# A shorter quotient for the FFN weight, value products behind the scores of a later item, projections and joint norms two slots later

## The chip, the cores and the metric

The kernel runs on one core of one Trainium2 chip, in one launch. The metric is the device time of one execution in microseconds (us); lower is better. PE is the matrix engine, DVE the vector engine, ACT the scalar engine, POOL the GpSimd engine; SP is the engine that issues nearly all DMAs here.

## What is computed

x has shape (4, 4096, 512) in float32. Three residual steps follow one another:

```python
x = x + 0.5 * ffn(layernorm(x))
x = x + attention(layernorm(x))
x = x + 0.5 * ffn(layernorm(x))
```

`ffn` quantises its input and its 512 x 512 weight in blocks of 32 to a 6-bit grid (scale = largest absolute value / 7.5, nearest grid value, ties to the lower one), multiplies the dequantised matrices and adds a bias:

```python
scales = maximum(max(abs(blocks), -1) / 7.5, 1e-30)
q = nearest_on_grid(blocks / scales)
out = (xq * xs) @ (wq * ws).T + bias
```

`attention` has 16 heads of 32 and a window of 13 neighbours (clipped at the ends of the sequence) with a relative position bias per head; it projects to q, k and v, takes the softmax of q k + bias over the 13 neighbours, multiplies by v and projects the result with `proj_w`.

## The kernel before

The 16384 rows are cut into 128 tiles of 128 rows. Every product with a weight is done with both operands split into a high and a low float16 half; `product` (L152) issues 12 matmuls of 128 x 512 for it. The weights sit transposed in `wt`, put there in a setup that quantises the FFN weight `fw` and splits all weights.

Four tiles make a group; a group and a quarter of the heads make an item, so there are 128 items too, and a tile and an item take the same number of steps. The steps are:

- `first_half(t)`: the first FFN product (`pmf`), its addition to x on DVE (L280), the statistics of the second norm (L181), its factors on POOL, the normalised tile on ACT, its low half on DVE and a transposing DMA into `x2` (L206).
- `values(t)`: the v product (`pmv`), which goes to DRAM (L317) and comes back as stacks of overlapping windows (`load_stack`, L441).
- `project_qk(m)`: two products (`pmqk`); DVE subtracts the high halves (L391), ACT spreads q (L398).
- `softmax(m)`: 64 to 72 small matmuls for the scores (`ps`, L466), then DVE, POOL and ACT in turn; in the end the probabilities are transposed by a DMA (`pT`, L535).
- `attend(m)`: the value products (`pv`, L557), 64 to 72 small matmuls; their result goes to a ring of rows (L584 on ACT, L590 on DVE).
- `project_out(t)`: the product `pmo` from the ring, its addition to x (L603) and the statistics of the third norm.
- `quantised_norms(slot)`: the norm and quantisation ahead of an FFN product. It runs for one tile, or jointly for two, the third norm of a tile and the first norm of the tile 15 further on. Its stages, one per slot: factors (POOL, L187 to L196), normalised tile (ACT, L234), block scales (DVE, L240 to L245), scaling (POOL, L247), rounding to 8 bits (ACT, L250), scaling back (POOL, L252), high half (ACT, L201), low half (DVE, L205) with the transposing DMA to `xT` (SP, L206).
- `second_half(t)`: the second FFN product (a `pmf` again, from `xT`), its addition (L280) and the store (L609).

The order on every engine is written out by hand. Time is cut into slots; a step is entered into a slot with a rank, and goes on in a later slot with the rank that its `yield` names. Within a slot the lower rank comes first, and equal ranks in the order of entry. Each engine executes its instructions in that order; the setup alone is ordered by a planner, up to the point where the manual order begins. Tile t and item m are `STEP` = 7 slots behind their predecessors:

```python
for _, stage in sorted(slots.pop(slot, ()), key=lambda e: e[0]):
    for n, rank in stage:
        begin(slot + n, stage, rank)
        break
```

The results of products share three PSUM banks in turn (`ps_m`); scores have four banks, value products one. The last tiles have slots of their own (`out_slot`, `second_slot`), and eight second halves (`HELD`) are kept back for the end.

Of the kernel before, what the change touches and what calls it, by code (L numbers as in the profile page):

```python
# [37 lines left out]
P = 128  # L38
# [12 lines left out]
QB = 32  # L51
Q_MAX = 7.5
Q_EPS = 1e-30
LN_EPS = 1e-5

F8_SCALE = 64.0
BELOW_ONE = 1.0 - 2.0 ** -24
MASKED = -1e38
XS = 4.0
PS = 1024.0  # L60
# [4 lines left out]
def macaron_kernel(  # L65
# [25 lines left out]
    const = ctx.enter_context(tc.tile_pool(name="const", bufs=1))  # L91
# [13 lines left out]
    nudge = const.tile([P, 1], F32, name="nudge")  # L105
    nc.gpsimd.memset(nudge, -(2.0 ** -28) * (1 + 2.0 ** -10))

    least = const.tile([P, 2 * NB], F32, name="least")
    nc.vector.memset(least, F8_SCALE * XS * Q_EPS)
    p_scale = const.tile([P, MAXB], F32, name="p_scale")  # L110
# [26 lines left out]
    def tie_to_lower(t):  # L137

        nc.vector.scalar_tensor_tensor(t, t, BELOW_ONE, t, ALU.mult, ALU.min)
        ti = t.bitcast(I32)
        nc.vector.tensor_scalar(ti, ti, 1, None, ALU.bitwise_or)

    def product(pm, lhs, rhs):

        n = 0
        for a, b in ((0, 1), (1, 0), (0, 0)):  # L150
            for c in range(KC):
                nc.tensor.matmul(  # L152
                    pm, lhs(a, c), rhs(b, c), start=(n == 0), stop=(n == 3 * KC - 1)
                )
                n += 1
# [7 lines left out]
    def begin(slot, stage, rank=5):  # L163
        slots.setdefault(slot, []).append((rank, stage))
# [185 lines left out]
    def row_of(h):  # L350

        return h // 2 * 2 * QR + h % 2

    n_items = n_batch * NG * KC
# [240 lines left out]
    def project_out(t, slot):  # L595

        r = t * P % RING
        pm = ps_m.tile([P, dim], F32, tag="mm", name=f"pmo_{t}")
        product(
            pm, lambda s, c: ring[:, s, c, r : r + P], lambda s, c: wt[:, s, c, PO : PO + dim]  # L600
        )
        yield 1, 8
        nc.vector.scalar_tensor_tensor(xs[t], pm, cp, xs[t], ALU.mult, ALU.add)  # L603
        moments(slot, t, "n3")

    def second_half(t):

        yield from ffn(t, "f2")
        nc.sync.dma_start(out=of[t * P : (t + 1) * P, :], in_=xs.pop(t))  # L609


    EARLY = 3
    STEP = 7

    F1, V, QK, SC, PV, OUT, F2 = 5, 2 * STEP + 6, 5 * STEP + 3, 6 * STEP, 8 * STEP + 3, 13 * STEP + 2, 12

    def add_bias(t, b):
        nc.gpsimd.tensor_tensor(xs[t], xs[t], b, ALU.add)  # L618
# [1 line left out]
    def one(f, *args):  # L620
        f(*args)
        return
        yield
# [3 lines left out]
    HELD = range(NT - 15, NT - 7)  # L627
    LAST = NT - GROUP - 1

    def out_slot(t):  # L630


        i = t - LAST
        if i >= 0:
            return (n_items - 1) * STEP + PV + 3 + 2 * i
        if i >= 1 - GROUP:
            return LAST * STEP + PV + 21 + 4 * i
        return t * STEP + OUT

    def second_slot(t):  # L640

        i = t - LAST
        if t in HELD:
            return (n_items - 1) * STEP + PV - (16, 13, 10, 6, 5, 4, 3, 2)[t - HELD[0]]
        if i in (-2, -1):
            return out_slot(NT - 1) + 3 + i
        return out_slot(t) + F2

    for t in range(NT):
        k = t * STEP  # L650
        sooner = (0, 2, 5, STEP)[t] if t <= EARLY else 0
        begin(k - 18 - (STEP if t == EARLY else 0), one(load, t), 0)
        slot = k - 10 - (10 if t == EARLY else 0)
        enlist(slot, t, "n1")
        if not 0 < t < EARLY:
            begin(slot - 1, one(moments, slot, t, "n1"), 1)
        begin(k + F1 - sooner, first_half(t))
        begin(k + V, values(t))
        begin(k + F1 - sooner, one(add_bias, t, half_ffn_b), 8)
        at = out_slot(t)  # L660
        begin(at - 5, one(add_bias, t, after_b), 8)
        enlist(at + 2, t, "n3")
        begin(at, project_out(t, at + 2))
        begin(at + 6 if t < LAST else second_slot(t) - 2, one(add_bias, t, half_ffn_b), 8)
        begin(second_slot(t), second_half(t))
    for slot in together:
# [2 lines left out]
    for m in range(n_items):  # L669
        k = m * STEP  # L670
        begin(k + QK, project_qk(m))
        begin(k + SC, softmax(m), 6)
        begin(k + PV, attend(m), 6)
    for n in range(n_batch * NG):
        k = n * GROUP * STEP
        b, g = divmod(n, NG)
# [4 lines left out]
    with tc.tile_pool(name="setup", bufs=1) as sp, tc.tile_pool(name="scratch", bufs=2) as scr:  # L681
        ident = sp.tile([P, P], F32, name="ident")
        make_identity(nc, ident)
        fw = sp.tile([P, KC, dim], F32, name="fw")
# [20 lines left out]
        for o in chunks:  # L705
            w, i = (qkv_w, o) if o < 3 * KC else (proj_w, o - 3 * KC)
# [14 lines left out]
        up = sp.tile([P, 5], F32, name="up")  # L721
# [40 lines left out]

        def small(name):
            return sp.tile([P, KC * NB], F32, name=name)

        w_abs, w_sc, w_hi, w_lo, w_r = (
            small(s) for s in ("w_abs", "w_sc", "w_hi", "w_lo", "w_r")
        )  # L770

        def split_scale():
            nc.vector.tensor_scalar(
                w_hi.bitcast(I32), w_sc.bitcast(I32), -4096, None, ALU.bitwise_and
            )
            nc.vector.tensor_tensor(w_lo, w_sc, w_hi, ALU.subtract)
# [17 lines left out]
        def large(name, o, dt=F32):  # L794
            return scr.tile(
                [P, NB, QB], dt, tag=name, bufs=3 if name == "wu_" else KC, name=f"{name}{o}"
            )

        for o in range(KC):
            fwb = blocks(fw[:, o, :])  # L800

            def per(t):
                return bc(t[:, o * NB : (o + 1) * NB], QB)
# [12 lines left out]
            nc.scalar.activation(  # L816
                w8.rearrange("p n q -> p (n q)"), q0f, AF.Copy, scale=1.0 / F8_SCALE,
                saturate=False,
            )
# [64 lines left out]
        for turned in (0, 2):  # L884
            for h in range(4):
                at = row_of(h ^ turned)
# [41 lines left out]
        slot = first  # L928
# [49 lines left out]
```

## Time and profile before

| | us |
|---|---|
| median of 3 runs | 2313.0 |
| lowest and highest | 2311.24, 2313.52 |
| the profiled execution, its time | 2312.25 |
| its span, first to last instruction | 2310.5 |
| PE busy | 2211.1 (96%) |
| DVE busy | 2044.8 (88%) |
| POOL busy | 1988.3 (86%) |
| ACT busy | 1695.5 (73%) |

Busy times are sums over one profiled execution. Matmuls overlap, so the length shown for a row of matmuls ends a little after the next row may start; distances from start to start are the better measure. A line number is that of the kernel's source, and an arrow `<-` in brackets names what ended a wait.

### The profile page before, as it was taken

How to read it: one execution, taken by the hardware profiler on the slowest of the kernel's cores; microseconds unless marked ns; L12 is line 12 of the kernel's file. 1: busy time of each engine (PE TensorE's matmuls, PEld its weight loads, DVE VectorE, ACT ScalarE, POOL GpSimd, SP SyncE). 2: the span in 40 equal slices, each digit the busy share in tenths (PEclk: the TensorE clock that was granted, in tenths of full speed). 3: DMA queues.
4: the chain of work that ended last, by engine and by line, in shares of the span. 5: the costliest groups of instructions: out<-in, count | busy, mean ns of one | idle time of the engine just before them, and what ended most of it. 6: DMA issues, size and time to landing. Idle time of an engine off the chain costs nothing.

```text
span 2310.5 us, 65475 instructions
## 1 busy us (share of the span) xinstructions
PE 2211.1 (96%) x26771; PEld 1052.0 (46%) x26771; DVE 2044.8 (88%) x3797; ACT 1695.5 (73%) x2544; POOL 1988.3 (86%) x2017
## 2 busy tenths in 40 slices
PE   0799999999999999999999999999999999999978
PEld 0244444444444444444444444444444444444433
DVE  8799998998988989989989899899898998998775
ACT  4588777777777777777777777777777777777752
POOL 6488988888988888888888898888898889888776
PEclk9999999999999999999999999999999999999999
DMA  5788888788877888888878888888787888887764
GB/s 153 156 167 160 162 162 159 156 163 162 154 158 157 158 163 157 160 161 159 158 156 160 158 160 166 155 154 161 159 159 157 160 158 165 156 157 148 138 109 107
DMA packets 926213, 359.61 MB, mean 156 GB/s; under 512 B 719452, under 2 KB 890328, under 8 KB 925912
## 3 DMA queue, kind: packets, MB, share of 16 engines
q1 hardware_dynamic: 925568, 354.90, 79.3%
q8 instruction: 209, 3.42, 0.6%
q14 instruction: 92, 0.75, 0.1%
q10 hardware_dynamic: 344, 0.53, 0.1%
HBM read 110.26 MB, written 67.29 MB: 77 GB/s over the span
## 4 chain that ended last, share of the span: by engine, by line
PE 89%; DVE 6%; POOL 2%; ACT 1%; DMA 1%; issue 1%; SPq 0%; POOLq 0%; DVEq 0%; ACTq 0%
PE pmqk L152 28%; PE pmf L152 27%; PE pmo L152 14%; PE pmv L152 13%; PE ps L466 4%; PE pv L557 3%; DVE stn L181 1%; DVE hlq L205 0%; ACT qk L398 0%; DVE sc L240 0%; DVE x L280 0%; DVE fw L810 0%; DVE hln L205 0%; DVE whl L840 0%; DMA fw<-in_L_ffn_weight_dram 0%
## 5 line engine op out<-in xcount | busy, mean ns | idle before, releaser
L152 PE MATMUL pmf<-wt,xT 128*128 128x512 f16 x3048 | 701.3, 380 | 9.0 <-DMA xT<-hlq 7.7
L152 PE MATMUL pmqk<-x,wt 128*128 128x512 f16 x3072 | 705.8, 379 | 0.3 <-DVE after_b L876 0.3
L152 PEld LDWEIGHTS <-xT 128*128 128x128 f16 x3048 | 297.9, 98 | 372.7 <-DMA xT<-hlq 13.1
L152 PEld LDWEIGHTS <-wt 128*128 128x128 f16 x3072 | 289.7, 98 | 335.6 <-issue 0.9
L247 POOL TENSOR_TENSOR yq<-yq,r 128x1024 f32<-128x1024 f32 (+1 forms) x141 | 247.1, 1753 | 133.9 <-DVE r L245 120.4
L152 PE MATMUL pmv<-wt,x 128*128 128x512 f16 x1536 | 354.0, 380 | 6.0 <-DMA x<-hln 3.3
L152 PE MATMUL pmo<-wt,ring 128*128 128x512 f16 x1536 | 356.1, 382 | 0.0
L398 ACT ACTIVATE qk<-qf,parity 128x1024 f16<-128x1024 f16 x256 | 349.3, 1431 | 0.0
L618 POOL TENSOR_TENSOR x<-x,half_ffn_b 128x512 f32<-128x512 f32 x256 | 327.7, 1280 | 0.0
L280 DVE SCALAR_TENSOR_TENSOR x<-pmf,coef,x 128x512 f32<-128x512 f32 x256 | 179.8, 702 | 144.5 <-PE pmf L152 142.2
L584 ACT ACTIVATE ring<-pv 128x510 f16<-128x510 f32 (+7 forms) x176 | 78.7, 475 | 297.6 <-PE pv L557 229.1
L181 DVE BATCH_NORM_STATS2 stn<-x 128x6 f32<-128x512 f32 x384 | 265.2, 691 | 8.9 <-DMA x<-in_L_attn_x_dram 0.2
L252 POOL TENSOR_TENSOR yq<-q,sc 128x1024 f32<-128x1024 fp8e4 (+1 forms) x141 | 246.6, 1749 | 1.5 <-ACT q L250 1.5
L152 PEld LDWEIGHTS <-x 128*128 128x128 f16 x1536 | 150.5, 98 | 188.9 <-issue 5.0
L250 ACT ACTIVATE q<-yq,nudge 128x1024 fp8e4<-128x1024 f32 (+1 forms) x141 | 150.0, 1064 | 116.7 <-POOL yq L247 108.5
L152 PEld LDWEIGHTS <-ring 128*128 128x128 f16 x1536 | 141.0, 98 | 159.9 <-issue 3.9
L526 POOL TENSOR_TENSOR sf<-sf,total 128x714 f32<-128x714 f32 (+2 forms) x128 | 178.7, 1396 | 37.1 <-ACT yq L234 21.6
L234 ACT ACTIVATE yq<-x,nbq,rsq 128x512 f32<-128x512 f32 x254 | 193.0, 803 | 17.1 <-POOL nbq L193 14.4
L533 POOL TENSOR_TENSOR p<-sf,p 128x714 f16<-128x714 f32 (+2 forms) x128 | 192.5, 1504 | 0.0
L517 POOL TENSOR_TENSOR sf<-sf,top 128x714 f32<-128x714 f32 (+2 forms) x128 | 181.5, 1418 | 3.8 <-DVE top L515 3.6
L205 DVE TENSOR_TENSOR hlq<-yq,hlq 128x1024 f16<-128x1024 f32 (+1 forms) x141 | 170.6, 1210 | 8.1 <-ACT hlq L201 6.9
L618 POOL TENSOR_TENSOR x<-x,after_b 128x512 f32<-128x512 f32 x128 | 162.4, 1269 | 0.0
(155 smaller groups left out, 3494.4 us busy)
## 6 DMA issues: line engine op xcount, KB each, us to landing
vs<-vd SPq DMA_DIRECT2D x144, 357.0 KB
x<-in_L_attn_x_dram SPq DMA_DIRECT2D x128, 256.0 KB
vd<-vt SPq DMA_DIRECT2D x128, 256.0 KB
out_dram<-x SPq DMA_DIRECT2D x128, 256.0 KB
vs<-vd SPq DMA_DIRECT2D x24, 378.0 KB
vs<-vd SPq DMA_DIRECT2D x24, 315.0 KB
rows<-in_L_attn_qkv_w_dram SPq DMA_DIRECT2D x12, 256.0 KB
xT<-hlq SPq DMA_TRANSPOSE x141
```

The costliest lines, as they stand in the source:

```text
L152: nc.tensor.matmul(pm, lhs(a, c), rhs(b, c), start=(n == 0), stop=(n == 3 * KC - 1))
L181: nc.vector.bn_stats(st, xs[t])
L205: nc.vector.tensor_tensor(hl[:, :, 1, :], y, hl[:, :, 0, :], ALU.subtract)
L234: nc.scalar.activation(y[:, u], xs[t], AF.Identity, bias=nb[:, u : u + 1], scale=rs[:, u : u + 1])
L247: nc.gpsimd.tensor_tensor(yb, yb, bc(r, QB), ALU.mult)
L252: nc.gpsimd.tensor_tensor(yb, q8.rearrange("p u (n q) -> p (u n) q", q=QB), bc(sc, QB), ALU.mult)
L280: nc.vector.scalar_tensor_tensor(xs[t], pm, cf, xs[t], ALU.mult, ALU.add)
L398: nc.scalar.activation(to, whole[0], AF.Copy, scale=parity[:, e : e + 1])
L517: nc.gpsimd.tensor_tensor(s, s, bc(top[:, :n], KN), ALU.subtract)
L526: nc.gpsimd.tensor_tensor(s, s, bc(total[:, :n], KN), ALU.mult)
L533: nc.gpsimd.tensor_tensor(p[:, :n, KN : 2 * KN], s, ph, ALU.subtract)
L618: nc.gpsimd.tensor_tensor(xs[t], xs[t], b, ALU.add)
```

## The change

In the setup the quotient of the FFN weight is shortened. Before, it was built from a reciprocal, a float16 first guess and two corrections with split scales, and ties were moved to the lower value by integer operations. After, the weight is multiplied by the reciprocal of its scale, and a small negative bias in ACT's rounding decides the ties; the multiplication back is on DVE and no longer on POOL.

In the order, with slots counted from 7 x the number of the tile or item: the value products of an item go from slot 59 to slot 63, which is the slot of the scores of the item three ahead, with a rank behind them (the last three items stay at 59). `project_out` goes from slot 93 to 95 with rank 7 in place of 5; `second_half` stays 12 slots behind it. The joint norms go two slots later as well (the first norm of a tile from slot -10 to -8), so the two norms stay together. For the last tiles the constants are rewritten so that most of them keep their slots.

```diff
+    w_nudge = const.tile([P, 1], F32, name="w_nudge")
+    nc.gpsimd.memset(w_nudge, -(2.0 ** -27) * (1 + 2.0 ** -10))
...
-    F1, V, QK, SC, PV, OUT, F2 = 5, 2 * STEP + 6, 5 * STEP + 3, 6 * STEP, 8 * STEP + 3, 13 * STEP + 2, 12
+    F1, V, QK, SC, PV, OUT, F2 = 5, 2 * STEP + 6, 5 * STEP + 3, 6 * STEP, 9 * STEP, 13 * STEP + 4, 12
+
+    LAST_PV = (n_items - 1) * STEP + 8 * STEP + 3
...
-            return (n_items - 1) * STEP + PV + 3 + 2 * i
+            return LAST_PV + 3 + 2 * i
         if i >= 1 - GROUP:
-            return LAST * STEP + PV + 21 + 4 * i
+            return LAST * STEP + 82 + 4 * i
...
-            return (n_items - 1) * STEP + PV - (16, 13, 10, 6, 5, 4, 3, 2)[t - HELD[0]]
+            return LAST_PV - (16, 13, 10, 6, 5, 4, 3, 2)[t - HELD[0]]
...
-        slot = k - 10 - (10 if t == EARLY else 0)
+        slot = k - (8 if t > EARLY else 18 if t == EARLY else 10)
...
-        begin(at, project_out(t, at + 2))
+        begin(at, project_out(t, at + 2), 7)
...
         begin(k + SC, softmax(m), 6)
-        begin(k + PV, attend(m), 6)
+        begin(k + (PV if m < n_items - 3 else PV - 4), attend(m), 7)
...
         for o in range(KC):
             nc.vector.tensor_reduce(
-                w_abs[:, o * NB : (o + 1) * NB], blocks(fw[:, o, :]), AX.X, ALU.max,
+                w_sc[:, o * NB : (o + 1) * NB], blocks(fw[:, o, :]), AX.X, ALU.max,
                 apply_absolute_value=True,
             )
-        nc.vector.tensor_scalar(w_sc, w_abs, 1.0 / Q_MAX, None, ALU.mult)
-        split_scale()
-        nc.vector.scalar_tensor_tensor(w_abs, w_hi, -Q_MAX, w_abs, ALU.mult, ALU.add)
-        nc.vector.scalar_tensor_tensor(w_abs, w_lo, -Q_MAX, w_abs, ALU.mult, ALU.add)
-        nc.vector.scalar_tensor_tensor(w_sc, w_abs, 1.0 / Q_MAX, w_sc, ALU.mult, ALU.add)
-        nc.vector.tensor_scalar(w_sc, w_sc, Q_EPS, None, ALU.max)
+        nc.vector.tensor_scalar(
+            w_sc, w_sc, F8_SCALE / Q_MAX, F8_SCALE * Q_EPS, ALU.mult, ALU.max
+        )
         nc.vector.reciprocal(w_r, w_sc)
-        split_scale()
-        w_back = small("w_back")
-        nc.vector.tensor_scalar(w_back, w_sc, up[:, 4:5], F8_SCALE, ALU.mult, ALU.mult)
...
         for o in range(KC):
             fwb = blocks(fw[:, o, :])
-            qh, q0 = large("wqh_", o, F16), large("wq0_", o)
-            nc.vector.tensor_tensor(qh, fwb, per(w_r), ALU.mult)
-            for i, b in enumerate((w_hi, w_lo)):
-                u = large("wu_", f"{o}_{i}")
-                nc.gpsimd.tensor_tensor(u, qh, per(b), ALU.mult)
-                nc.vector.tensor_tensor(fwb, fwb, u, ALU.subtract)
-            nc.vector.tensor_tensor(q0, fwb, per(w_r), ALU.mult)
-            nc.vector.tensor_tensor(q0, q0, qh, ALU.add)
-            q0f = q0.rearrange("p n q -> p (n q)")
-            tie_to_lower(q0f)
-            w8 = large("w8_", o, F8)
-            nc.scalar.activation(
-                w8.rearrange("p n q -> p (n q)"), q0f, AF.Copy, scale=1.0 / F8_SCALE,
-                saturate=False,
-            )
-            nc.gpsimd.tensor_tensor(fwb, w8, per(w_back), ALU.mult)
+            nc.vector.tensor_tensor(fwb, fwb, per(w_r, o), ALU.mult)
+        nc.vector.tensor_scalar(w_back, w_sc, up[:, 4:5], None, ALU.mult)
+        for o in range(KC):
+            w8 = scr.tile([P, dim], F8, tag="w8_", bufs=KC, name=f"w8_{o}")
+            nc.scalar.activation(w8, fw[:, o, :], AF.Identity, bias=w_nudge, saturate=False)
+            nc.vector.tensor_tensor(blocks(fw[:, o, :]), blocks(w8), per(w_back, o), ALU.mult)
             hl = scr.tile([P, 2, dim], F16, tag="whl", bufs=4, name=f"whlf{o}")
             nc.scalar.copy(hl[:, 0, :], fw[:, o, :])
             nc.vector.tensor_tensor(hl[:, 1, :], fw[:, o, :], hl[:, 0, :], ALU.subtract)
```

`tie_to_lower` was one DVE operation that multiplied by a number just below one and took the minimum (L143) and one that set the lowest bit (L145).

More of the change, by code (lines that the diff above doesn't have):

```diff
@@ L56 @@
 F8_SCALE = 64.0
-BELOW_ONE = 1.0 - 2.0 ** -24
 MASKED = -1e38
@@ L135, in blocks @@
         return t.rearrange("p (n q) -> p n q", q=QB)
[L137 to L145, printed above, removed]
     def product(pm, lhs, rhs):
@@ L761, in put_weights @@
             )
[L765 to L769, printed above, removed]
-        )
-        def split_scale():
-            nc.vector.tensor_scalar(
-                w_hi.bitcast(I32), w_sc.bitcast(I32), -4096, None, ALU.bitwise_and
-            )
-            nc.vector.tensor_tensor(w_lo, w_sc, w_hi, ALU.subtract)
+        w_sc, w_r, w_back = (
+            sp.tile([P, KC * NB], F32, name=name) for name in ("w_sc", "w_r", "w_back")
+        )
@@ L787, in macaron_kernel @@
-        nc.vector.scalar_tensor_tensor(w_sc, w_abs, 1.0 / Q_MAX, w_sc, ALU.mult, ALU.add)
-        nc.vector.tensor_scalar(w_sc, w_sc, Q_EPS, None, ALU.max)
-        nc.vector.reciprocal(w_r, w_sc)
-        split_scale()
-        w_back = small("w_back")
-        nc.vector.tensor_scalar(w_back, w_sc, up[:, 4:5], F8_SCALE, ALU.mult, ALU.mult)
[L794 to L797, printed above, removed]
+        nc.vector.tensor_scalar(
+            w_sc, w_sc, F8_SCALE / Q_MAX, F8_SCALE * Q_EPS, ALU.mult, ALU.max
+        )
@@ L799, in macaron_kernel, with per @@
+        nc.vector.reciprocal(w_r, w_sc)
+        def per(t, o):
+            return bc(t[:, o * NB : (o + 1) * NB], QB)
         for o in range(KC):
             fwb = blocks(fw[:, o, :])
-            def per(t):
-                return bc(t[:, o * NB : (o + 1) * NB], QB)
-            qh, q0 = large("wqh_", o, F16), large("wq0_", o)
-            nc.vector.tensor_tensor(qh, fwb, per(w_r), ALU.mult)
-            for i, b in enumerate((w_hi, w_lo)):
-                u = large("wu_", f"{o}_{i}")
-                nc.gpsimd.tensor_tensor(u, qh, per(b), ALU.mult)
-                nc.vector.tensor_tensor(fwb, fwb, u, ALU.subtract)
@@ L811, in macaron_kernel @@
-            nc.vector.tensor_tensor(q0, fwb, per(w_r), ALU.mult)
-            nc.vector.tensor_tensor(q0, q0, qh, ALU.add)
-            q0f = q0.rearrange("p n q -> p (n q)")
-            tie_to_lower(q0f)
-            w8 = large("w8_", o, F8)
-            nc.scalar.activation(
-                w8.rearrange("p n q -> p (n q)"), q0f, AF.Copy, scale=1.0 / F8_SCALE,
-                saturate=False,
-            )
-            nc.gpsimd.tensor_tensor(fwb, w8, per(w_back), ALU.mult)
+            nc.vector.tensor_tensor(fwb, fwb, per(w_r, o), ALU.mult)
```

## The prediction

> **What bounds the kernel now.** I read the page's busy shares first, then the engines' busy time by stretch, then PE's timeline over one item, then DVE's and SP's for the same item, and last the chain at both ends of the span.
>
> ```profile
> PE 2211.1 (96%) x26771; PEld 1052.0 (46%) x26771; DVE 2044.8 (88%) x3797; ACT 1695.5 (73%) x2544; POOL 1988.3 (86%) x2017
> ```
> ```profile
> 0.00:40.00 40.00, 1.55 (x5) 0.84 (x5) 32.53 (x70) 18.34 (x48) 27.46 (x49) 1.00 0.54 181
> ...
> 1000.00:1400.00 400.00, 400.00 (x4907) 191.18 (x4906) 359.35 (x662) 303.17 (x444) 356.94 (x352) 1.00 0.82 159
> ```
>
> From 260 to 2160 us PE is busy in every microsecond and its waits in that window are none. DVE has 90% there, POOL 89%, the DMA engines 82%. So the middle is PE's, with little to spare elsewhere; only the first 60 us (PE works for 3 of them) and the last 150 us wait for others. One item on PE (columns: start, length, engine, line, operation, out<-in):
>
> ```profile
> 1002.02 0.81 PE L466 MATMUL ps<-qk 64*64 64x84 f16 x68
> 1002.76 2.76 PE L152 MATMUL pmo<-wt,ring 128*128 128x512 f16 x12
> 1005.36 2.75 PE L152 MATMUL pmqk<-x,wt 128*128 128x512 f16 x12
> 1008.05 0.69 PE L557 MATMUL pv<-pT,vs 126*32 126x30 f16 x68
> 1008.67 2.76 PE L152 MATMUL pmqk<-x,wt 128*128 128x512 f16 x12
> 1011.27 2.75 PE L152 MATMUL pmf<-wt,xT 128*128 128x512 f16 x12
> 1013.86 2.75 PE L152 MATMUL pmv<-wt,x 128*128 128x512 f16 x12
> 1016.45 2.75 PE L152 MATMUL pmf<-wt,xT 128*128 128x512 f16 x12
> 1019.14 0.80 PE L466 MATMUL ps<-qk 64*64 64x84 f16 x68
> ```
>
> Start to start, a product of 12 matmuls takes 2.59 to 2.60; in front of scores (ps) or value products (pv) it takes 2.69, so entering the small tiles costs 0.09. Scores take 0.74, value products 0.62. An item is 1019.14 - 1002.02 = 17.12, or 17.11 by the mean of its neighbours. The first pmf is first_half, the second is second_half, 15 tiles behind.
>
> DVE in the same item, and the landing of a joint norm's transpose (SP's issue, and the product that waited for it in the ramp):
>
> ```profile
> 1002.13 0.75 DVE L280 SCALAR_TENSOR_TENSOR x<-pmf,coef,x 128x512 f32<-128x512 f32 x1 [1.19 <-PE pmf L152]
> ...
> 1006.50 0.72 DVE L603 SCALAR_TENSOR_TENSOR x<-pmo,coef,x 128x512 f32<-128x512 f32 x1
> 1007.25 0.69 DVE L181 BATCH_NORM_STATS2 stn<-x 128x6 f32<-128x512 f32 x1
> 1007.98 0.18 DVE L182 BATCH_NORM_AGGREGATE mv<-stn 128x2 f32<-128x6 f32 x1
> 1008.08 1.21 DVE L205 TENSOR_TENSOR hlq<-yq,hlq 128x1024 f16<-128x1024 f32 x1
> ...
> 1013.46 0.74 DVE L391 SCALAR_TENSOR_TENSOR qk<-pmqk,qk_b,qk 128x512 f16<-128x512 f32 x1
> ```
> ```profile
> 223.62 2.06 SPq L206 DMA_TRANSPOSE xT<-hlq  x1
> ```
> ```profile
> 228.11 2.76 PE L152 MATMUL pmf<-wt,xT 128*128 128x512 f16 x12 [0.36 <-DMA xT<-hlq]
> ```
>
> DVE runs its program in order. The low half of a joint norm (L205, hlq) stands directly behind L603 and its statistics, and L603 waits for this item's pmo. So already now each xT leaves only after the newest pmo. From pmo's end (1005.36) to the second_half that needs that xT (1016.45) PE has 11.1 us of other work, and that hides the chain. The transpose of two tiles landed 228.11 - 223.62 = 4.49 after its issue.
>
> **The change, part by part.**
>
> *Order in the steady stage.* Worked out from the slots and ranks, a slot being a seventh of an item. PE before: scores, pmo, pmqk, pv, pmqk, pmf (first half), pmv, pmf (second half). After: scores, pv, pmf (second half), pmqk, pmqk, pmo, pmf (first half), pmv. One of two entries into small tiles goes from behind a full product to behind scores. The full entry costs 0.09; scores to value products is nowhere in this trace, so its price lies between 0 and 0.09, and below nothing isn't excluded but small, as 68 scores leave for pmo at no visible cost (1002.02 + 0.74). I take 0.03, nearer to nothing because the small matmuls in front are short. Without waits an item would take 17.11 - 0.06 = 17.05.
>
> The page "TensorEngine Tiling (Array Packing)" of the Trainium skill, section Tiling Modes, says that a change of tiling mode drains the array; scores (64*64) and value products (126*32) are different modes, so by the rule the saving is nothing, and the sum would be 113 x 0.06 = 7 us higher.
>
> *The norm that feeds second_half.* Here a cover goes. In the new order project_out stands in slot 4 behind the second pmqk; L603 and the statistics follow in slot 5 with rank 8; in slot 6 come the second L391 with rank 0 and then, rank 1, L205 on hlq with its transpose on SP; second_half is in slot 2 of the next item. Slot distances are kept, but not what PE does in them: from pmo's end to second_half there are now pmf 2.59, pmv 2.60, the entry 0.09, scores 0.74, entry 0.03, pv 0.62 = 6.67 us, not 11.1. The chain across the same stretch: pmo's end to L603's start 0.20 (L280 starts 0.11 after the scores' start, which is 0.09 behind the product's end); L603 and statistics 1.58 (1006.50 to 1008.08); L391 0.70; L205 1.21; issue 0.03; landing 4.49. Sum 8.21, and 0.10 for a collision with POOL, whose factors for the next norm become ready just then. POOL's small L187 took 1.08 beside L205 and 0.19 without it, and its longest piece (L190) is 0.57 without it; so the collision costs L205 between 0 and 0.57, and I take a low value because L391 lies between. That makes 8.31.
>
> It is a loop of one item: pmo, L603, L205, transpose, second_half, two pmqk, pmo. The four products are 4 x 2.59 = 10.37, so the loop lasts 18.68 against 17.11 now: +1.57 an item, a wait of 8.31 - 6.67 = 1.64 of PE before each second_half. Nothing else waits behind that xT on SP. It happens for as many items as have a two-tile norm: the group L205 on 128x1024 counts 113. 113 x 1.57 = +177 us.
>
> The unsure term is the landing, 113 us for each microsecond of it. Lower end: a one-tile transpose near the end, issued at 2294.59, released PE at 2297.69, 3.1. Upper end: the median issue in the view of tile xT is 2971 ns, 0.91 more than the 2.06 above, so 5.4. I take 4.49, measured on the same size. In the new order pT's transpose is no longer directly in front, which speaks for the lower side; the loads of vs are, which speaks for the upper.
>
> The page "SBUF — State Buffer", section "SBUF: two separate sides", says that a VectorE operation with two SBUF inputs and a GpSimd operation exclude each other for a whole instruction. By this rule L205 pays up to all of L190, 0.47 more than I took, and the sum would be 53 us higher.
>
> *Value products and the rest of the item.* pv's transposed probabilities and its stack of values are now issued more than an item before their use, longer than before, so pv itself waits for nothing. The ring's rows reach pmo after three products (7.8 us) at the worst tile; copy and subtraction take 0.6 each: hidden, unless ACT or DVE lag by 6 us. The biases on POOL move with their steps, with no new user in PE's way.
>
> *Setup.* Removed on DVE: L806 2.5, eight L810 8.6, L811 5.3, L812 3.6, L143 3.9, L145 2.5 and eight operations on 64 columns 1.6 = 28.0; on POOL eight L809 and four L820. Added on DVE: eight products of 512 columns, 0.68 each alone and 1.53 beside POOL, so 5.4 to 12.2. Net 16 to 23. The chain of the first 60 us runs mostly through DVE (L810, L143, L145, L812), and the first product starts behind it:
>
> ```profile
> 58.97 4.33 PE L152 MATMUL pmf<-wt,xT-10_168 128*128 128x512 f16 x12 [16.64 <-DMA wt<-whlf]
> ```
>
> I take -18, with 8 to 23 as bounds, since the attention weights that come next may not move as far.
>
> *Ramp.* Norms start two slots later for tiles past the third, and their ACT copy now stands in front of the L398 pair that the scores wait for. Items last 11 to 12 us there; about 0.6 (one copy) for nine items: +5, bounds 0 and 10.
>
> *Tail.* With no first halves left, scores wait for ACT:
>
> ```profile
> 2203.78 1.31 PE L466 MATMUL ps<-qk 64*64 64x84 f16 x72 [4.09 <-ACT qk L398]
> ```
>
> Five such waits, 1.51, 1.51, 4.09, 4.09 and 1.50, sum to 12.7. pmo now stands between pmqk and scores and covers 2.59 of the first four: 0, 0, 1.5, 1.5 and 1.5 are left, -8; bounds -12 (PE's clock, 0.87 there, recovers too) and 0 (the last items' softmax ends last anyway).
>
> **Sum**, against the profiled execution (2312.25, span 2310.5): +177 - 18 + 5 - 8 = +156, 2468. The median of the runs shown is 0.75 higher: 2469.
>
> **The rivals.** *Faster.* The transpose lands in time and only the gains are left: 128 x 0.06 = 8, 18 and 8 less 5, so 2313 - 29 = 2284. It decides if xT lands within 4.49 - 1.64 = 2.85 us; even half the data took 3.1. Against it too: L205 can't pass L603. For it: a scheduler that did not keep the written order, but the trace shows the slots' order on every engine.
>
> *The PSUM bank instead.* If xT comes in time, pmv reuses the bank of the second pmqk, three products back, which L391 frees 0.20 + 1.58 + 0.70 = 2.48 after pmo; pmv is due at 2.59. A late L603 then costs up to 0.5 an item: 2284 + 56 = 2340.
>
> *Still slower.* The landing is 5.4: 113 x 0.91 = 103 more, 2572. The DMA engines at 82% speak for it.
>
> **How the numbers follow.** Main case 0.70, still slower 0.18, bank 0.06, faster 0.06. What can be told from no change is about 0.2%, 4.6 us. Of the faster case 0.05 is beyond that and 0.01 within; the other cases are slower, 0.94. Range: landing near 3.9 with the best ends of setup and tail gives 2400; the still slower case gives 2572, so 2400 to 2575; it leaves out the two small cases.
>
> **What would show it.** Right: pmf of second_half waits for xT in nearly every item, 1.2 to 2.5 us; PE below 93%; the first pmf near 41 us; scores' waits in the tail halved; pv behind scores and no wait before pv. Wrong: an item of 17.1 or less, or PE waiting in the steady stage for anything but xT.

## The result, and the profile after

The changed kernel takes 2413.4 us (median; 2409.2 to 2415.8) against 2312.4 for the kernel before: 1.0435 times as long, 95% interval 1.0417 to 1.0453. The forecast was 2469, range 2400 to 2575, slower with 0.94. The profiled execution took 2415.8, its span 2414.0.

The page's busy shares, and the same middle stretch as before (length; busy time of PE, PEld, DVE, ACT and POOL; granted clock; DMA share; GB/s):

```profile
PE 2216.8 (92%) x26771; PEld 1066.4 (44%) x26771; DVE 2038.4 (84%) x3769; ACT 1706.6 (71%) x2544; POOL 1934.1 (80%) x2006
```
```profile
1000.00:1400.00 400.00, 378.30 (x4595) 182.56 (x4594) 345.47 (x627) 287.93 (x414) 329.11 (x331) 1.00 0.67 150
```

PE stands still for 21.7 of 400 us where it never did, at a granted clock of 1.00, and every other engine works less too, so none of them has become the bound. The waits of PE (in all us, times, longest) name one cause above all, and the one-item timeline shows where it sits:

```profile
PE pmf L144 <- DMA xT<-hlq: 122.4, 116, 9.1
```
```profile
1104.20 0.81 PE L458 MATMUL ps<-qk 64*64 64x84 f16 x68
1104.94 0.69 PE L549 MATMUL pv<-pT,vs 126*32 126x30 f16 x68
1106.47 2.76 PE L144 MATMUL pmf<-wt,xT 128*128 128x512 f16 x12 [0.84 <-DMA xT<-hlq]
1109.07 5.34 PE L144 MATMUL pmqk<-x,wt 128*128 128x512 f16 x24
1114.25 2.75 PE L144 MATMUL pmo<-wt,ring 128*128 128x512 f16 x12
1116.84 2.75 PE L144 MATMUL pmf<-wt,xT 128*128 128x512 f16 x12
1119.43 2.75 PE L144 MATMUL pmv<-wt,x 128*128 128x512 f16 x12
1122.11 0.81 PE L458 MATMUL ps<-qk 64*64 64x84 f16 x68
1122.85 0.69 PE L549 MATMUL pv<-pT,vs 126*32 126x30 f16 x68
1124.41 2.76 PE L144 MATMUL pmf<-wt,xT 128*128 128x512 f16 x12 [0.87 <-DMA xT<-hlq]
```

The order is the one derived in the prediction. An item is 17.9 instead of 17.11, and the wait of 0.84 to 0.87 stands in front of second_half. DVE and SP between that pmo and that pmf:

```profile
1117.11 0.75 DVE L595 SCALAR_TENSOR_TENSOR x<-pmo,coef,x 128x512 f32<-128x512 f32 x1 [1.16 <-PE pmo L144]
1117.89 0.69 DVE L173 BATCH_NORM_STATS2 stn<-x 128x6 f32<-128x512 f32 x1
1118.62 0.18 DVE L174 BATCH_NORM_AGGREGATE mv<-stn 128x2 f32<-128x6 f32 x1
1118.72 0.72 DVE L383 SCALAR_TENSOR_TENSOR qk<-pmqk,qk_b,qk 128x512 f16<-128x512 f32 x1
1119.36 1.22 DVE L197 TENSOR_TENSOR hlq<-yq,hlq 128x1024 f16<-128x1024 f32 x1
```
```profile
1120.60 1.62 SPq L198 DMA_TRANSPOSE xT<-hlq  x1
```

(Lines have moved up by 8 or more: L595 was L603, L383 was L391, L197 was L205.) The loop is the one forecast, link for link: pmo's end (where the next product starts) 1116.84, addition 1117.11, second L383 1118.72, low half 1119.36, issue 1120.60, product 1124.41. The links are 0.27, 1.61, 0.64, 1.24 and 3.81, in sum 7.57; the forecast had 8.31. The cover up to the end of the value products, 1116.84 to about 1123.5, is 6.7 as forecast.

In the setup and the ramp:

```profile
36.74 4.27 PE L144 MATMUL pmf<-wt,xT-10_170 128*128 128x512 f16 x12
```

The first product came at 58.97 before. The first scores came at 114.84 and now at 97.96; the first second_half of the steady stage at 228.11 and now at 220.58. The second half of the 113th tile started at 2146.02 and now starts at 2248.67. So the 103.5 us between the two spans are:

| stage | before | after | difference | forecast |
|---|---|---|---|---|
| start to first scores (setup) | 114.8 | 98.0 | -16.9 | -18 |
| to the first second_half (ramp) | 113.3 | 122.6 | +9.3 | +5 |
| 112 items | 1917.9 (17.12 each) | 2028.1 (18.11 each) | +110.2 | +177 |
| from there to the end (tail) | 164.4 | 165.4 | +0.9 | -8 |

### The profile page after: what moved, and what is told of

It is laid out like the page before. It is cut to its first block, busy times and chain, and to the rows that moved or that the text cites. A ratio compares the mean times of both kernels' runs of the same rounds, so it can differ in the third digit from the quotient of the medians.

```text
span 2414.0 us, 65764 instructions
## 1 busy us (share of the span) xinstructions
PE 2216.8 (92%) x26771; PEld 1066.4 (44%) x26771; DVE 2038.4 (84%) x3769; ACT 1706.6 (71%) x2544; POOL 1934.1 (80%) x2006
## 4 chain that ended last, share of the span: by engine, by line
PE 45%; DVE 17%; DMA 17%; POOL 10%; issue 7%; ACT 4%; DVEq 0%; SPq 0%; POOLq 0%; ACTq 0%
PE pmqk L144 22%; DMA xT<-hlq 15%; PE pmf L144 12%; PE pmo L144 11%; DVE x L595 4%; DVE stn L173 4%; DVE qk L383 3%; POOL x L612 2%; POOL sf L509 2%; POOL yq L244 2%; POOL yq L239 2%; ACT qk L390 1%; DVE sc L232 1%; DVE hlq L197 1%; POOL p L525 1%
## 5 line engine op out<-in xcount | busy, mean ns | idle before, releaser
L144 PE MATMUL pmf<-wt,xT 128*128 128x512 f16 x3048 | 711.3, 384 | 127.7 <-DMA xT<-hlq 122.4
L144 PE MATMUL pmqk<-x,wt 128*128 128x512 f16 x3072 | 687.0, 380 | 0.4 <-issue 0.4
L144 PEld LDWEIGHTS <-wt 128*128 128x128 f16 x3072 | 299.9, 98 | 362.4 <-issue 4.8
L612 POOL TENSOR_TENSOR x<-x,half_ffn_b 128x512 f32<-128x512 f32 x256 | 376.9, 1473 | 0.0
L390 ACT ACTIVATE qk<-qf,parity 128x1024 f16<-128x1024 f16 x256 | 350.2, 1433 | 0.0
L179 POOL TENSOR_SCALAR rsq<-mv 128x2 f32<-128x2 f32 (+1 forms) x141 | 28.2, 200 | 254.9 <-DVE mv L174 253.9
L595 DVE SCALAR_TENSOR_TENSOR x<-pmo,coef,x 128x512 f32<-128x512 f32 x128 | 95.8, 749 | 144.0 <-PE pmo L144 117.6
L193 ACT CAST hlq<-yq 128x1024 f16<-128x1024 f32 (+1 forms) x141 | 135.2, 959 | 101.3 <-POOL yq L244 96.4
L272 DVE SCALAR_TENSOR_TENSOR x<-pmf,coef,x 128x512 f32<-128x512 f32 x256 | 189.6, 741 | 18.2 <-PE pmf L144 15.9
L197 DVE TENSOR_TENSOR hln<-yn,hln 128x512 f16<-128x512 f32 x128 | 190.6, 1489 | 1.8 <-ACT hln L193 1.8
L379 ACT ACTIVATE qf<-pmqk,qk_b 128x512 f16<-128x512 f32 x128 | 87.7, 685 | 147.7 <-PE pmqk L144 146.1
```

The source lines that it names most:

```text
L144: nc.tensor.matmul(pm, lhs(a, c), rhs(b, c), start=(n == 0), stop=(n == 3 * KC - 1))
L197: nc.vector.tensor_tensor(hl[:, :, 1, :], y, hl[:, :, 0, :], ALU.subtract)
L272: nc.vector.scalar_tensor_tensor(xs[t], pm, cf, xs[t], ALU.mult, ALU.add)
L390: nc.scalar.activation(to, whole[0], AF.Copy, scale=parity[:, e : e + 1])
```

## Experiments

### Setup alone, order alone

The first kernel is the changed one with the slots and ranks of before. The second is the opposite: the new slots and ranks with the old setup.

```diff
-    ... SC, PV, OUT, F2 = ... 6 * STEP, 9 * STEP, 13 * STEP + 4, 12
+    ... SC, PV, OUT, F2 = ... 6 * STEP, 8 * STEP + 3, 13 * STEP + 2, 12
...
-            return LAST * STEP + 82 + 4 * i
+            return LAST * STEP + 80 + 4 * i
...
-        slot = k - (8 if t > EARLY else 18 if t == EARLY else 10)
+        slot = k - 10 - (10 if t == EARLY else 0)
...
-        begin(at, project_out(t, at + 2), 7)
+        begin(at, project_out(t, at + 2))
...
-        begin(k + (PV if m < n_items - 3 else PV - 4), attend(m), 7)
+        begin(k + PV, attend(m), 6)
```

> The order of before with the short quotient of after. Theory (the order costs, the setup gains): in the changed kernel the first product started 22.2 us sooner (36.74 against 58.97) but the first scores only 16.9 sooner (97.96 against 114.84) and the first pmo 8.2 sooner; if the 8.7 us lost between these two belong to the new order, this kernel keeps about 16 of them: 2296. Rival (the ramp is held by something that does not move with the setup): it keeps no more than 8: 2304 or more. Items in the middle stay at 17.11 in both.

Measured: 2293.3 us, ratio 0.9916 [0.9899, 0.9932]. Items are 17.11 to 17.12, the first scores stand at 96.28. So the shorter quotient gives 18.6 us up to the first scores, where 18 was forecast, and with the old order they are kept to the end (19.8). No other kernel run here is as quick.

> The changed kernel's order with the setup of before. It asks why the joint norm's transpose is 0.7 us quicker than forecast: the median issue of it on SP was 2971 ns in before, 1706 with before's order and the short setup, 1607 in the changed kernel. Theory (the order: the transpose no longer stands behind pT's): issue 1.6 and items of 17.9 to 18.0 here too, and only the setup's 20 us come on top, 2430 to 2437. Rival (the setup: with the old one the DMA engines spend more time on the same bytes, 79.3% of the span in before against 70.9% with the short one): issue well above 1.6 and a landing longer by 0.3 to 0.9, 113 us for each microsecond, so 2465 to 2530.

Measured: 2588.5 us, ratio 1.1196 [1.1151, 1.1241]: both expectations fell short, the order's by far. An item of it, and the transpose that it waits for:

```profile
1112.94 0.72 PE L557 MATMUL pv<-pT,vs 126*32 126x30 f16 x68
1115.31 2.76 PE L152 MATMUL pmf<-wt,xT 128*128 128x512 f16 x12 [1.65 <-DMA xT<-hlq]
```
```profile
1110.69 1.81 SPq L206 DMA_TRANSPOSE xT<-hlq  x1
```

Here the landing is 1115.31 - 1110.69 = 4.62, the wait 1.65 (the prediction: 4.49 and 1.64), and the median item 18.79 (the prediction: 18.68). The mean item between 260 and 2200 us is 19.48, because 29 of 99 last 20 to 23: a landing that is later still, and products at half speed behind some of these waits:

```profile
1056.61 5.30 PE L152 MATMUL pmf<-wt,xT 128*128 128x512 f16 x12 [3.11 <-DMA xT<-hlq]
```

So the two parts are not additive. Alone they make +276 and -20, together +101. The setup's edit takes 20 us off the start, and with the new order some 155 us more, out of the items. What it changes there is the transposes. Median landing of the joint norm's transpose in the steady stage, by the completion marks in the trace, with the median issue on SP behind it (the view of tile xT):

| | setup of before | short setup |
|---|---|---|
| order of before | 5.3 us (2971 ns) | 4.4 us (1706 ns) |
| new order | 4.6 us (1884 ns) | 3.7 us (1607 ns) |

The new order takes 0.7 off, and the short setup 0.9. On 113 items 0.9 is about 100 of the 155 us; the rest goes with the longer items and the slow products in some of them. In the order of before the transpose of `pT` stands directly ahead on SP, in the new one it does not. The same bytes also cost the DMA engines less time under the short setup. The page's DMA queue, kernel before and then setup alone (packets, MB, share of the span):

```profile
q1 hardware_dynamic: 925568, 354.90, 79.3%
```
```profile
q1 hardware_dynamic: 925568, 354.90, 70.9%
```

The difference is in packets of 256 bytes, which make up three quarters of the number: with the short setup more than nine in ten take 18 ns or less, in every kernel here; with the old setup the 90th percentile is 31 ns (before) and 33 (order alone), and the mean 25.0 and 23.2 against 20.7 (setup alone) and 20.1 (changed). Why a setup should do that for the whole run is not shown. One candidate is placement. The added constant `w_nudge` takes 32 bytes of each partition and moves every later tile: hlq's steady buffer lies at byte 126944 of the partition without it and at 126976 with it, which is 256 x 496, and the buffers of xT and p move in the same way from 32 bytes below a multiple of 256 onto one (pT's onto a multiple of 64). By the 90th percentile every kernel here with the constant has the quicker packets, both without it the slower. But a kernel with a constant of that size and nothing else was not run, so this stays an inference.

### Is it the cover? Second_half later, second_half in front

In both only the slot of second_half moves in the changed kernel, by 7 (a whole item, shown) or by 5 (in front of the scores); the joint norm stays where it is.

```diff
-        return out_slot(t) + F2
+        return out_slot(t) + F2 + (7 if t < HELD[0] else 0)
```

> The changed kernel with second_half of the tiles before the held ones 7 slots later, so that the order on PE within an item stays and only the tile changes: the transpose of its norm gets a whole item more of cover. Theory (PE waits for xT because L197 of the norm stands behind L595, which stands behind pmo): the waits for xT vanish, an item takes 17.02 to 17.05 in place of 17.93 to 18.08, and the whole 2415 - 112 x 1.05 = about 2297. Rival (a loop over the norm's stages on POOL and ACT, or the bank of the second pmqk, holds an item at 17.5 or more anyway): 2350 or more. Rival (the waits only move, to scores or pmv): the sum of PE's waits stays above 100 us and the time near 2410.

> As the one before, but second_half only 5 slots later: it comes into the slot of the scores, in front of them, as in the kernel of before, one entry into small tiles per item less than there. Theory: no wait for xT; an item 17.02; the scores get one product more between them and the second pmqk, so their waits for L390 in the tail and the ramp, about 14 us and 4 us in the changed kernel, do not grow; about 2297. Rival (what matters is that the scores follow on pmv and not the cover of xT): no different from the changed kernel, 2410.

Measured: 2302.6 us (0.9956 [0.9941, 0.9971]) and 2303.3 (0.9958 [0.9944, 0.9973]). With the item's delay PE no longer waits for xT between 260 and 2130 us, and most items last 17.01. Two starts of second_half there, and what runs just ahead of the second:

```profile
1157.74 2.76 PE L144 MATMUL pmf<-wt,xT 128*128 128x512 f16 x12
...
1173.38 0.74 PE L458 MATMUL ps<-qk 64*64 64x84 f16 x64
1174.10 0.69 PE L549 MATMUL pv<-pT,vs 126*32 126x30 f16 x68
1174.62 0.21 PE L549 MATMUL pw<-pT,vs 126*32 126x30 f16 x4
1174.76 2.76 PE L144 MATMUL pmf<-wt,xT 128*128 128x512 f16 x12
```

Giving the chain its cover back returns the 110 us of the steady stage: the wait for xT is the cause of the loss. It also prices the entry from scores into value products: 17.01 is 0.10 under 17.11, so the whole entry is saved. In the changed kernel too scores last 0.74 up to the value products (1104.20 to 1104.94), as they did up to pmo before.

The rest of it was not expected. These 2302 us are 9 above the setup alone, though the item is shorter. Where scores and value products adjoin, PE waits inside the value products for nothing that the profile shows, here in the kernel with the item's delay:

```profile
1104.76 0.56 PE L549 MATMUL pv<-pT,vs 126*32 126x30 f16 x52
1106.38 0.27 PE L549 MATMUL pv<-pT,vs 126*32 126x30 f16 x16 [1.06 <-issue]
```

To try that, the value products went back to their old slot and rank, with second_half still an item later. As the last tile of a group then reads ring rows that a later group has begun to overwrite, part of the output of every fourth tile differs.

```diff
-        begin(k + (PV if m < n_items - 3 else PV - 4), attend(m), 7)
+        begin(k + PV - 4, attend(m), 6)
```

> e2 with the value products back at slot 59, between the two pmqk; second_half stays an item later. It isolates the place of the value products. Theory (one entry from a full product into small tiles saved per item is worth 0.09 to 0.10): an item takes 17.11 in place of 17.01, so 120 x 0.10 = 12 us slower from this. Second theory (scores and value products in a row, 272 PE instructions in 1.4 us, are what PE's waits put down to issue come from: 12.6 us in e2, 0.7 in e1): these waits vanish, about 12 us faster. Together about 2302, with every item at 17.11 and no waits put down to issue. Rival (these waits are chance): they stay and the time is 2312 or more.

Measured: 2309.7 us, 0.9987 [0.9978, 0.9997]. Items are mostly 17.11 again, with about one of 18.5 in sixteen (pmqk there waits 1.3 for L272). The waits put down to issue:

| | before | setup alone | changed | second_half later | the same, value products apart |
|---|---|---|---|---|---|
| us in all | 0.3 | 0.7 | 7.4 | 12.6 | 0.7 |

In the other kernels that have the value products beside the scores these waits come to 2 to 11 us. So in the kernel with second_half later the place beside the scores gains 0.10 an item, 11 us, and loses about 12 to these waits: by this account it is worth about nothing. That the kernel with the value products apart is 7 us slower fits its six long items (1.4 each). What PE waits for in these places isn't shown.

### The transpose's neighbours

The joint norm's transpose is sent twice in the changed kernel, first into a buffer that nobody reads.

```diff
-        low(y, hl, xT[:, :n].rearrange("p u s c q -> p (u s c) q"))
+        if n == 2:
+            xD = xtp.tile([P, 2, 2, KC, P], F16, tag="xT", name=f"xD{slot}")
+            low(y, hl, xD.rearrange("p u s c q -> p (u s c) q"))
+            nc.sync.dma_start_transpose(
+                out=xT.rearrange("p u s c q -> p (u s c) q"),
+                in_=hl.rearrange("p u s k -> p (u s k)"),
+            )
+        else:
+            low(y, hl, xT[:, :n].rearrange("p u s c q -> p (u s c) q"))
```

> The changed kernel with the transpose of a joint norm sent twice in a row, first into a spare buffer and then into xT. In the kernel of before this transpose stood directly behind that of pT and took 4.4 to 5.4 us from issue to landing; in the changed one it stands alone and takes 3.7. Theory (the neighbour on the queue, not the size, made up the 0.7 that my landing was too long by): from the issue of the second to its landing 4.4 to 5.4, and with the first one's issue of 1.6 in front the loop is 2.3 to 3.3 longer: items of 20.2 to 21.2, the time 2413 + 112 x 2.3 to 3.3 = 2671 to 2783. Rival (the queue takes the second at the pace of the first): landing 3.7, only the 1.6 added, 2590.

Measured: 3066.1 us, 1.3262 [1.3242, 1.3281], a miss in size. SP, and the product behind:

```profile
1123.31 1.64 SPq L198 DMA_TRANSPOSE xD<-hlq  x1
1124.99 1.92 SPq L263 DMA_TRANSPOSE xT<-hlq  x1
```
```profile
1130.32 5.30 PE L144 MATMUL pmf<-wt,xT 128*128 128x512 f16 x12 [4.01 <-DMA xT<-hlq]
```

The second transpose lands 1130.32 - 1124.99 = 5.33 after its issue, where one alone takes 3.8, and starts 1.68 later: 3.2 us an item, as expected. The rest is PE's clock (0.869 in the mean): behind a wait of 4 us the product takes 5.1 instead of 2.6. 17.9 + 3.2 + 2.5 is 23.6 of the 23.9 that its items last. So a transpose directly behind another lands 1.5 later even with the short setup. That a neighbour ahead makes the order's share in the table above (0.7, behind the transpose of `pT`) fits this, but was not run by itself.

### Shorter loop: the second L383 ahead of L595

The second L383 stands in the loop (0.64). In the next kernel it is entered on its own, ahead of the addition L595.

```diff
-        put_low(1)
+        LOWS[m] = put_low
...
+        begin(k + QK + 2, one(lambda m: LOWS.pop(m)(1), m), 7)
```

> The changed kernel with the second L383 (0.64 us from its start to that of L197) moved ahead of L595 on DVE; everything else stays. Theory (the loop pmo, L595, statistics, L383, L197, transpose, second_half, two pmqk, pmo sets the item): the loop is 0.64 shorter, so an item takes 17.3 in place of 17.93 and the whole about 2413 - 112 x 0.64 = 2341; PE's wait for xT falls from about 0.9 to 0.25 an item. Rival (the landing of the transpose is set by the load on the DMA engines or by the norm's earlier stages, not by when L197 runs): less than a third of that, 2390 or more.

Measured: 2508.8 us, 1.0844 [1.0828, 1.0861]: a miss, even in sign. Its SP shows why:

```profile
1086.45 1.10 SPq L434 DMA_DIRECT2D vs<-vd  x2
1089.86 3.10 SPq L198 DMA_TRANSPOSE xT<-hlq  x1
```
```profile
1096.51 4.02 PE L144 MATMUL pmf<-wt,xT 128*128 128x512 f16 x9 [3.62 <-DMA xT<-hlq]
```

pmo's end is 1086.18 here. The loads of vs go out 0.3 behind it, where in the changed kernel they went out 2.0 ahead of it (1114.80 against 1116.84), so the transpose follows them by 3.4 instead of 5.8. Its issue takes 3.10 and it lands after 6.65. To remove that, the loads start later, once with the L383 in front and once, as a control, without it.

```diff
-        begin(k + 6 * STEP + 4, load_stack(b, g, 0), 9)
-        begin(k + 8 * STEP + 4, load_stack(b, g, 1), 9)
+        begin(k + 7 * STEP, load_stack(b, g, 0), 9)
+        begin(k + 9 * STEP, load_stack(b, g, 1), 9)
```

> e4 with the loads of the stacks (vs) three slots later, so that SP issues them behind xT and not in front of it. In e4 the transpose took 3.65 us from issue to landing where it went out 5.7 us behind one load, and 6.61 where it went out 2.8 us behind two; PE then sat idle for 3.62 us and its next product ran at half the clock (5.30 in place of 2.60). Theory (the loop is 0.64 shorter, and only the loads in front of the transpose spoilt that): every item takes about 17.3, the time is about 2413 - 112 x 0.64 = 2341. Rival (L383 ahead of L595 itself costs, by the order on DVE): near e4, 2480 or more.

> The changed kernel with only the loads of the stacks three slots later. Control for e5. Theory (in the changed kernel xT goes out 5.2 to 5.8 us behind the loads and already lands in 3.7): no gain in the item, 2405 to 2415; a few single items of 18.3 to 18.7 may come down to 17.9. Rival (the loads hold the transpose in the changed kernel as well): 2390 or less.

Measured: 2402.0 us (1.0388 [1.0372, 1.0403]) and 2409.9 (1.0422 [1.0405, 1.0439]). The control changes nothing that can be told from 2413; the loads cost something, 107 us, only where the transpose runs into them. But the L383 in front brings 8 us against this control (11 against the changed kernel), not 72. DVE says where the rest went:

```profile
1109.48 0.74 DVE L384 SCALAR_TENSOR_TENSOR qk<-pmqk,qk_b,qk 128x512 f16<-128x512 f32 x1
1110.15 0.73 DVE L596 SCALAR_TENSOR_TENSOR x<-pmo,coef,x 128x512 f32<-128x512 f32 x1
```

pmo's end is 1109.39. The addition (L596 here) starts 0.76 later instead of 0.27, because the L383 in front of it is itself late, behind the sums of the softmax (L515 to L517). So 0.49 of the 0.64 is only shifted to another place in the same queue; in the median of this kernel the addition starts 0.82 behind pmo's end, and the transpose goes out 0.11 sooner than in the changed kernel.

### Ramp and tail: the copy in front of the spread

In the tail the changed kernel's scores wait 14.0 us in five places, where the forecast had left 4.5. Of these 11.4 are put down to the spread L390 on ACT, in front of which the norm's high half (L193) waits for POOL. The next two kernels move that copy behind the spread, with second_half an item later and without.

```diff
-        yield 1, 3
+        yield 2, 1
         ...
         high(y, hl)
-        yield 1, 1
```

> The changed kernel with second_half one item later (2302.6 us alone), and the norm's high-half copy on ACT moved behind the spread (L390) that the scores wait for. Theory on ramp and tail: the scores' waits for L390 (13.6 us there in 12 waits, of which 9.4 in the tail) come from that copy, which waits for POOL. Then the ramp's seven waits of about 0.5 go (-4) and the tail's shrink by the copy and its wait for POOL, 0.6 to 1.4 in each of four (-2 to -6): 2293 to 2297. Rival: the spread is late because of the product and DVE's part in front of it; then the waits stay at 13 and the time at 2302 to 2304.

> The changed kernel with only the norm's high-half copy on ACT moved behind the spread (L390). In the steady stage the chain from pmo to the transpose runs through DVE's L595 and low half, not through this copy, as long as the copy ends before the low half may start. Theory: steady item unchanged at 17.9 to 18.0, ramp and tail shorter by 6 to 10 us: 2403 to 2408. Rival 1: the copy, now later, becomes the last thing the low half waits for; each 0.1 us of that costs 11 us, so 0.5 would give 2460. Rival 2: nothing moves, 2411 to 2415.

Measured: 2307.6 us (0.998 [0.997, 0.9989]) and 2419.8 (1.0455 [1.0432, 1.0478]): the first a little worse than with second_half's delay alone (2302.6), the second not clearly different from the changed kernel, and neither gains. The ramp's items go from 11.9 to 13.0, and in the tail the scores now wait on DVE. Its rows in the first of the two, and the scores:

```profile
2194.81 0.74 DVE L594 SCALAR_TENSOR_TENSOR x<-pmo,coef,x 128x512 f32<-128x512 f32 x1
...
2196.42 0.72 DVE L382 SCALAR_TENSOR_TENSOR qk<-pmqk,qk_b,qk 128x512 f16<-128x512 f32 x1
```
```profile
2197.28 1.05 PE L457 MATMUL ps<-qk 64*64 64x84 f16 x72 [4.27 <-DVE qk L382]
```

The second L382 stands behind pmo's addition and its statistics, so two queues lead to the scores. The last kernel clears both: it has second_half an item later, the copy behind the spread, the L383 in front and the later loads.

> Second_half one item later, the norm's high-half copy behind the spread on ACT, the second half's L383 ahead of L595 on DVE, and the loads of vs behind the transpose (the edits of the three kernels before, in one). Two-queue theory of the tail: the scores wait for whichever is later, the spread behind ACT's copy or the second L383 behind DVE's L595 and statistics, so one edit alone uncovers the other; with both, each of the last four or five waits loses 1.0 to 1.6, and the tail's waits of the scores fall from 10.8 (copy behind alone) and 14.9 (L383 first alone) to 5 to 8; the time to 2301 to 2305 (the copy's cost in the ramp, 8 us, stays). Rival: the end is set by the product and the softmax before it; then these waits stay at 10 to 15 and the time at 2305 to 2310.

Measured: 2385.2 us, 1.0313 [1.0296, 1.033]. Both theories failed on the time, but on the tail the rival holds: with both queues cleared its scores still wait 13.9 us. ACT there:

```profile
2282.58 0.93 ACT L511 ACTIVATE sf<-sf,coef 128x756 f32<-128x756 f32 x1 [2.07 <-POOL sf L509]
2283.41 0.67 ACT L379 ACTIVATE qk<-pmqk,qk_b 128x512 f16<-128x512 f32 x1
2283.98 2.71 ACT L390 ACTIVATE qk<-qf,parity 128x1024 f16<-128x1024 f16 x2
```

The exponential of the preceding item (L511) waits for POOL and stands ahead of the copy of q and the spread; the scores follow at 2286.74. So tail items of 13 to 15 us look like a round through DVE, POOL and ACT, with PE's work hidden in it; no kernel here shortened that round, so this is read from the rows and not shown.

The steady stage of this kernel is slow too, at 17.75 an item, though xT has a whole item to spare:

```profile
1104.49 2.75 PE L144 MATMUL pmo<-wt,ring 128*128 128x512 f16 x12 [0.49 <-DVE x L271]
```

pmo waits for the PSUM bank that second_half's addition frees (34 us in 66 items, and pmqk for the ring's rows 20 us in 27). Neither wait shows in the kernel with the loads alone, nor in the two with the copy alone. They don't show in the two others with the L383 in front either, but there PE waits for xT, which can hide them. So the L383 in front, alone or together with another edit, is the candidate, and how the links of this second loop share the time was not taken apart.

## Why the prediction was right, and where it was not

**Mechanism and sign.** Right. The cover of 11.1 us fell to 6.7, the loop through pmo, L595, the second L383, the low half and the transpose became the bound, and PE waits at the named product. Moving only second_half gives all of it back. Two of the signs that were named failed: the wait is 0.85 and not 1.2 to 2.5, and the scores' waits in the tail were not halved (14.0 us against 12.7).

**The landing, 4.49.** This is the term that was mis-sized: it measured 3.81 in the row shown and 3.7 in the median. It is 0.7 of the 0.74 by which the loop was forecast too long, 113 x 0.7 = 79 us; the item's wait is 0.85 instead of 1.64. (That is +0.8 for the typical item of 17.9, or 90 of the 110 us; the mean of 18.11 holds longer ones as well, up to 22, for which the sum had no term.) The reason was not the one considered. The prediction asked whether pT's transpose or the loads would be in front of it, and took the size from a row with the old setup. With the old setup the figure holds in the new order (4.6 landed, 1.65 waited, items of 18.79). It is the setup's edit that makes this transpose land 0.9 sooner, a part that had been priced by its instructions alone; how it does so stays open. That the time lies in the range is partly luck. Without that side effect the change would have cost 276 us less the setup's 20, near the upper end. With it the landing came out under the 3.9 that stood for the lower end, and the longer items, the ramp and the tail made up for that.

**The entry, 0.03.** It was 0.00: an item without waits is 17.01, not 17.05. The issue waits beside it, 7.4 us in the changed kernel, had no term. A rule spoke against this saving: the Trainium skill, "TensorEngine Tiling (Array Packing)", section Tiling Modes, has a change of mode drain the array. Between these two small modes (64 x 64 and 126 x 32) no run here shows a price.

**POOL beside the low half, 0.10.** It was nothing: L197 has a median of 1215 ns with POOL beside it in every item, against 1206 for the same operation before (L205). POOL's product of mean and factor beside it (L187 here, L195 before, so not the L187 of the prediction) takes 0.67, where it took 0.20 clear of it before, so POOL pays. The exclusion that the Trainium skill states ("SBUF — State Buffer", section "SBUF: two separate sides") is visible, but not the 53 us on this path.

**Setup -18, ramp +5.** Measured -16.9 and +9.3, within their bounds. In the ramp the changed kernel also has one of the unexplained issue waits, 3.3 us long.

**Tail -8.** Measured +0.9, just past the bound of nothing. The reason that stood beside that bound, the softmax that ends last anyway, fits the rows of the last kernel.

**Rivals.** The faster case needed a landing under 2.85, and none was near that. Its 2284 was itself too low: with the wait gone the time is 2302.6, since the ramp takes 9, the tail gives nothing and the issue waits take 12. The bank did not decide in the changed kernel (pmv waits once, 0.5); PE waits for one in most items only in the last kernel, and there it is pmo that does.

## What to carry to other kernels

When a step moves, measure the chain between the moved step and its consumer against the work that is left between them; a transfer's landing is the least certain link, so take it as a range over its neighbours on the queue and over the kernel's other edits. Here an edit far away in the program went with quicker transfers in the whole run, for a reason that stayed open, so run each half of a two-part change alone before you add their prices. And taking one instruction out of a full engine's loop helps only if what stood in front of it was early.

## What the hardware showed that was not expected

Of the 256-byte packets more than nine in ten took 18 ns or less in every kernel with the short setup, while the 90th percentile with the long one was 31 and 33 ns; with it the same transpose landed 0.9 us later in the median. The placement of the tiles differs by 32 bytes, and whether that is the cause is open.

With the short setup a transpose of 128 x 2048 float16 landed in 3.8 us alone, in 5.3 directly behind another, and in 6.65 when issued 3.4 us behind the first of two loads. These neighbours don't explain every landing: in the last kernel its median was 5.2, 5.0 us behind the issue of a small transpose, and in the kernel with only the loads later 3.7, 5.8 us behind it.

With value products directly behind the scores, some 140 small matmuls in a row, PE sometimes stands still among the value products for up to 3.6 us without a releaser; with two large products between the two these waits are all but gone (0.3 to 0.7 us in a whole run).

In the kernel that sends the transpose twice, PE ran the product behind each wait of 3 to 6 us slowly, most at half speed (5.1 instead of 2.6 us from start to start). Behind the changed kernel's usual waits of 0.8 to 0.9 it kept 2.6, with one exception. Between the two lies no sharp line: with the order alone, some waits of 1.5 to 2 us were followed by a slow product and some of 3 were not.
